# Packing W and transposed x into single buffers, aligning chunks at their ends, loading x for two tiles at once, in a store-heavy pairwise bilinear kernel

**Chip, cores, metric.** One core of a Trainium2 chip. The metric is the device time of one execution in microseconds (us). Ratios are the mean time of one kernel's fast runs over the mean of the other's fast runs of the same rounds, so they are not quite the ratio of the medians quoted here. A run counts as slow when it is over 1.5% above the fastest run of the same kernel.

## The reference

```python
# x = r_inputs: (4096, 32, 64) f32;  W: (496, 64, 64) f32, one matrix for each pair i < j of the 32 fields
i_idx, j_idx = np.triu_indices(32, k=1)
vi, vj = x[:, i_idx, :], x[:, j_idx, :]
y = (jnp.einsum('bpd,pde->bpe', vi, W) * vj).reshape(4096, -1)     # (4096, 31744) f32: 520 MB
```

The output is some twelve times larger than everything that is read, so almost all of the traffic is stores.

## The kernel before

The batch goes through in 32 tiles of 128 rows (one row a partition). Fields are taken in 16 pairs p = (2p, 2p+1), which share TensorE's array: the even field's x lies transposed on partitions 0 to 63, the odd one's on 64 to 127. For each pair, chunks of up to 512 columns are multiplied into two PSUM banks. VectorE multiplies both banks by x in one instruction of two runs, into a ring buffer in SBUF that holds 0.89 of a tile. Four stores a tile empty the ring.

```python
STORES = [[0, 1], [2, 3], [4, 5, 6], [7, 8, 9, 10, 11, 12, 13, 14, 15]]
...
for c0 in range(0, width[2 * p], CHUNK):            # CHUNK = 512; the short chunk comes last
    n = [max(0, min(CHUNK, width[2 * p + h] - c0)) for h in range(2)]
    half = -(-n[0] // BANK) * BANK
    pm = take_banks(2 * half // BANK)
    ...                                             # the matmuls of both fields
    o = [off[2 * p + h] - o0 + c0 for h in range(2)]
    xj = [(2 * p + h + 1) * D + c0 for h in range(2)]
    if n[1] > half - BANK and o[1] + n[0] <= store_w[s]:
        nc.vector.tensor_tensor(                    # both fields at once, n[0] columns each
            runs(osb, o[0], o[1], n[0]), runs(pm, 0, half, n[0]), runs(xt, xj[0], xj[1], n[0]), ALU.mult)
    else:
        ...                                         # one instruction for each field
...
nc.sync.dma_start(out=out[ts(t, P), o0 : o0 + store_w[s]], in_=osb)
```

Of the kernel before, what the change touches and what calls it, by code (L numbers as in the profile page):

```python
# [1 line left out]

# [6 lines left out]

F32 = mybir.dt.float32  # L10
ALU = mybir.AluOpType

P = 128
BANK = 512
BANKS = 8
CHUNK = BANK

STORES = [[0, 1], [2, 3], [4, 5, 6], [7, 8, 9, 10, 11, 12, 13, 14, 15]]
PREFETCH_AT = [5, 6]
RING = 28160  # L20


@with_exitstack
def pair_bilinear_kernel(
    ctx: ExitStack,
    tc: tile.TileContext,
    x: bass.AP,
    w: bass.AP,
    out: bass.AP,
    F: int,  # L30
    D: int,
):




















    nc = tc.nc
    B = x.shape[0]
    NT = B // P
    NPR = F // 2

    width = [(F - 1 - i) * D for i in range(F)]
    off = [sum(width[:i]) for i in range(F)]
    woff = [sum(width[0 : 2 * p : 2]) for p in range(NPR)]  # L60
    store_w = [sum(width[2 * p] + width[2 * p + 1] for p in g) for g in STORES]

    const = ctx.enter_context(tc.tile_pool(name="const", bufs=1))
    xtpool = ctx.enter_context(tc.tile_pool(name="xT", bufs=2))
    psum = ctx.enter_context(tc.tile_pool(name="ps", bufs=1, space=bass.MemoryType.PSUM))

    ident = const.tile([P, P], F32, tag="ident", name="ident")
    make_identity(nc, ident)

    def runs(tl, a, b, n):  # L70

        ap = tl[:, a : a + n]
        return bass.AP(ap.tensor, ap.offset, [list(ap.ap[0]), [b - a, 2], list(ap.ap[1])])


    xbuf = [const.tile([P, (F + 1) * D], F32, tag=f"x{b}", name=f"x{b}") for b in range(2)]
    for xb in xbuf:
        nc.gpsimd.memset(xb[:, F * D :], 0.0)  # L78

    def load_x(t):  # L80
        xt = xbuf[t % 2]
        nc.scalar.dma_start(out=xt[:, : F * D], in_=x[ts(t, P), :])
        return xt

    pring = psum.tile([P, BANKS * BANK], F32, tag="pring", name="pring")
    bank = 0

    def take_banks(n):

        nonlocal bank  # L90
        if bank + n > BANKS:
            bank = 0
        got = pring[:, bank * BANK : (bank + n) * BANK]
        bank = (bank + n) % BANKS
        return got

    def transpose_x(xT, t, xt, g):

        n = 2 * BANK // P
        pt = take_banks(2)  # L100
        for c in range(n):
            nc.tensor.transpose(pt[:, ts(c, P)], xt[:, ts(n * g + c, P)], ident)  # L102
        nc.scalar.copy(xT[:, ts(g, 2 * BANK)], pt)  # L103

    def new_xT(t):
        return xtpool.tile([P, NPR * P], F32, tag="xT", name=f"xT_{t}")

    ring = const.tile([P, RING], F32, tag="ring", name="ring")
    at = 0
    xs = {0: load_x(0)}  # L110

    w_sb = []
    for p in range(NPR):
        wp = const.tile([P, width[2 * p]], F32, tag=f"w{p}", name=f"w{p}")
        nc.sync.dma_start(out=wp, in_=w[:, woff[p] : woff[p] + width[2 * p]])
        w_sb.append(wp)

    xTs = {0: new_xT(0)}
    for g in range(2):
        transpose_x(xTs[0], 0, xs[0], g)  # L120

    for t in range(NT):
        xt, xT = xs.pop(t), xTs.pop(t)
        if t + 1 < NT:
            xs[t + 1] = load_x(t + 1)
        for s, group in enumerate(STORES):
            if at + store_w[s] > RING:
                at = 0
            osb = ring[:, at : at + store_w[s]]
            at += store_w[s]  # L130
            o0 = off[2 * group[0]]
            for p in group:
                if t + 1 < NT and p in PREFETCH_AT:
                    if t + 1 not in xTs:
                        xTs[t + 1] = new_xT(t + 1)
                    transpose_x(xTs[t + 1], t + 1, xs[t + 1], PREFETCH_AT.index(p))
                for c0 in range(0, width[2 * p], CHUNK):
                    n = [max(0, min(CHUNK, width[2 * p + h] - c0)) for h in range(2)]
                    half = -(-n[0] // BANK) * BANK
                    pm = take_banks(2 * half // BANK)  # L140
                    for b0 in range(0, n[0], BANK):
                        b1 = min(b0 + BANK, n[0])
                        for h in range(2):
                            if b0 < n[h]:
                                nc.tensor.matmul(  # L145
                                    pm[:, h * half + b0 : h * half + b1],
                                    xT[h * D : (h + 1) * D, ts(p, P)],
                                    w_sb[p][h * D : (h + 1) * D, c0 + b0 : c0 + b1],
                                    start=True,
                                    stop=True,  # L150
                                )
                    o = [off[2 * p + h] - o0 + c0 for h in range(2)]
                    xj = [(2 * p + h + 1) * D + c0 for h in range(2)]
                    if n[1] > half - BANK and o[1] + n[0] <= store_w[s]:
                        nc.vector.tensor_tensor(  # L155
                            runs(osb, o[0], o[1], n[0]),
                            runs(pm, 0, half, n[0]),
                            runs(xt, xj[0], xj[1], n[0]),
                            ALU.mult,
                        )  # L160
                    else:
                        for h in range(2):
                            if n[h]:
                                nc.vector.tensor_tensor(  # L164
                                    osb[:, o[h] : o[h] + n[h]],
                                    pm[:, h * half : h * half + n[h]],
                                    xt[:, xj[h] : xj[h] + n[h]],
                                    ALU.mult,
                                )
            nc.sync.dma_start(out=out[ts(t, P), o0 : o0 + store_w[s]], in_=osb)  # L170


# [33 lines left out]
```

## Time and profile before

| | before |
|---|---|
| time, median of 3 runs | 1337.8 us (1337.75 to 1338.07) |
| VectorE busy | 1199.1 us (90%) |
| TensorE matmuls busy | 1154.1 us (86%) |
| VectorE waiting for stores to free the ring | 68.0 us |
| moved by DMA | 562.88 MB, mean 421 GB/s |

The page's lines, the waits and a tile's end are shown in the prediction below.

### The profile page before, as it was taken

To read this page: it belongs to the slowest core of one execution; us is meant where nothing else is said; L and a number is where in the kernel's file an instruction comes from. 1 tells how busy PE (TensorE), PEld (TensorE's weight loads), DVE (VectorE), ACT (ScalarE), POOL (GpSimd) and SP (SyncE) were. 2 spreads that over 40 slices of the span, in tenths; PEclk is the share of its full clock that TensorE was granted. 3 is DMA by queue.
4 is the path that set the end of the run, shared out by engine and by line. 5 is a ranking of instruction groups with operands and counts; after the bars stand their busy time and mean duration, and the time that the engine had idled before them with its cause. 6 is when DMAs were issued, how large, how long until landed. Compare 5 with 4: busy or idle time off the path is not lost. (4 is left out here: it accounts for less than half of the span.)

```text
span 1335.8 us, 13084 instructions
## 1 busy us (share of the span) xinstructions
PE 1154.1 (86%) x5376; PEld 529.9 (40%) x5376; DVE 1199.1 (90%) x1344; ACT 66.1 (5%) x65; POOL 0.9 (0%) x8
## 2 busy tenths in 40 slices
PE   7898898988888889898888898898988888888883
PEld 3343343433343444344334444343443333333331
DVE  5999898999899999899999899989988989999994
ACT  1000000000000000000000000000000000000000
POOL 0000000000000000000000000000000000000000
PEclk9999999899999999999999999999999999999997
DMA  9999999999999999999999999999999999999998
GB/s 392 435 426 431 436 408 434 415 426 431 419 417 425 428 429 416 418 424 420 424 436 419 418 421 426 424 426 421 418 430 414 426 423 413 424 427 430 418 420 370
DMA packets 25403, 562.88 MB, mean 421 GB/s; under 512 B 2944, under 2 KB 3328, under 8 KB 4864
## 3 DMA queue, kind: packets, MB, share of 16 engines
q1 hardware_dynamic: 20736, 528.49, 92.6%
q10 hardware_dynamic: 4608, 33.56, 6.0%
q8 instruction: 42, 0.69, 0.2%
q14 instruction: 17, 0.14, 0.0%
HBM read 41.94 MB, written 520.09 MB: 421 GB/s over the span
## 5 line engine op out<-in xcount | busy, mean ns | idle before, releaser
L155 DVE TENSOR_TENSOR ring<-pring,x 128x1024 f32<-128x1024 f32 (+3 forms) x1088 | 1154.2, 1107 | 116.9 <-DMA out_dram<-ring 68.0
L145 PE MATMUL pring<-w,xT 64*128 64x512 f32 (+4 forms) x4864 | 1087.8, 563 | 132.3 <-DVE ring L155 127.9
L145 PEld LDWEIGHTS pring<-w,xT 64*128 64x128 f32 x4864 | 472.9, 192 | 721.4 <-DVE ring L155 611.7
L103 ACT COPY xT<-pring 128x1024 f32<-128x1024 f32 x64 | 64.8, 1012 | 1197.1 <-PE pring L102 1197.1
L102 PE MATMUL pring<-ident,x 128*128 128x128 f32 x512 | 71.5, 285 | 30.7 <-DMA x<-in_x_dram 30.3
L102 PEld LDWEIGHTS pring<-ident,x 128*128 128x128 f32 x512 | 57.0, 144 | 65.6 <-issue 65.6
L164 DVE TENSOR_TENSOR ring<-pring,x 128x64 f32<-128x64 f32 (+4 forms) x256 | 70.9, 297 | 3.3
L103 ACT ACT_TABLE_LOAD x1 | 1.3, 1283 | 1.7 <-PEq L198 1.7
masks.py:199 POOL TENSOR_SCALAR_AFFINE_SELECT ident<-ident 128x128 f32<-128x128 f32 x1 | 0.3, 292 | 0.0
L78 POOL MEMSET x<- 128x64 f32 x2 | 0.2, 152 | 0.0
masks.py:197 POOL MEMSET ident<- 128x128 f32 x1 | 0.2, 204 | 0.3 <-POOLq L198 0.3
L198 POOL MEMSET const-bfloat16-1.0<- 128x1 bf16 x1 | 0.1, 101 | 0.0
L198 POOL MEMSET const-uint8-127<- 128x1 uint8 x1 | 0.1, 101 | 0.0
L198 POOL MEMSET const-float32-0.0<- 128x1 f32 x1 | 0.1, 98 | 0.2 <-issue 0.2
L198 POOL MEMSET const-float32-1.0<- 128x1 f32 x1 | 0.1, 98 | 0.0
## 6 DMA issues: line engine op xcount, KB each, us to landing
out_dram<-ring SPq DMA_DIRECT2D x32, 4896.0 KB, 18.6
out_dram<-ring SPq DMA_DIRECT2D x32, 3936.0 KB, 17.4
out_dram<-ring SPq DMA_DIRECT2D x32, 3776.0 KB, 19.0
out_dram<-ring SPq DMA_DIRECT2D x32, 3264.0 KB, 19.4
x<-in_x_dram ACTq DMA_DIRECT2D x32, 1024.0 KB, 17.8
w<-in_w_dram SPq DMA_DIRECT2D x1, 992.0 KB, 7.5
w<-in_w_dram SPq DMA_DIRECT2D x1, 928.0 KB, 11.8
w<-in_w_dram SPq DMA_DIRECT2D x1, 864.0 KB, 13.4
```

Of the source, the lines that this page charges most:

```text
L78: nc.gpsimd.memset(xb[:, F * D :], 0.0)
L102: nc.tensor.transpose(pt[:, ts(c, P)], xt[:, ts(n * g + c, P)], ident)
L103: nc.scalar.copy(xT[:, ts(g, 2 * BANK)], pt)
L145: nc.tensor.matmul(pm[:, h * half + b0 : h * half + b1], xT[h * D : (h + 1) * D, ts(p, P)], w_sb[p][h * D : (h + 1) * D, c0 + b0 : c0 + b1 ...
L155: nc.vector.tensor_tensor(runs(osb, o[0], o[1], n[0]), runs(pm, 0, half, n[0]), runs(xt, xj[0], xj[1], n[0]), ALU.mult,)
L164: nc.vector.tensor_tensor(osb[:, o[h] : o[h] + n[h]], pm[:, h * half : h * half + n[h]], xt[:, xj[h] : xj[h] + n[h]], ALU.mult,)
L198: nc = bacc.Bacc("TRN2", target_bir_lowering=False, num_devices=1)
```

## The change

It packs W into one SBUF buffer filled by five loads, keeps one transposed-x buffer whose two halves are refilled in turn (at pair 3 for the current tile, at pair 9 for the next), loads x for two tiles with one DMA, lays the batch out so that each partition owns 32 consecutive rows, and puts the short chunk of each pair first, so that all chunks end where the pair ends. With W's odd rows shifted by one block of zeros, both fields use the same columns of x. The intent is fewer, larger transfers and fewer exceptions in VectorE's work. The core of the diff:

```diff
-PREFETCH_AT = [5, 6]
+LOADS = [[0], [1], [2, 3], [4, 5, 6], [7, 8, 9, 10, 11, 12, 13, 14, 15]]
+FIRST_HALF_AT, SECOND_HALF_AT = 9, 3
+def x_slots(NT): ...                 # tile 0 alone, then pairs of tiles, in three slots of one buffer
-    for p in range(NPR):
-        wp = const.tile([P, width[2 * p]], F32, tag=f"w{p}", name=f"w{p}")
-        nc.sync.dma_start(out=wp, in_=w[:, woff[p] : woff[p] + width[2 * p]])
+    w_sb = const.tile([P, sum(width[0::2])], F32, tag="w", name="w")
+    for g in LOADS:
+        upto = woff[2 * g[-1]] + width[2 * g[-1]]
+        nc.sync.dma_start(out=w_sb[:, done:upto], in_=w[:, done:upto])
...
-                for c0 in range(0, width[2 * p], CHUNK):
+                first = (width[2 * p] - 1) % BANK + 1
+                for c1 in range(first, width[2 * p] + 1, BANK):
+                    n = first if c1 == first else BANK
+                    c0 = c1 - n
+                    odd = width[2 * p + 1] and c1 > D
...
+                    o = [off[2 * p + h] - o0 + c0 - h * D for h in range(2)]
+                    if odd and (c0 or c1 < width[2 * p]):
                         nc.vector.tensor_tensor(
-                            runs(xt, xj[0], xj[1], n[0]),
+                            bass.AP(xj.tensor, xj.offset, [xj.ap[0], [0, 2], xj.ap[1]]),
...
-            nc.sync.dma_start(out=out[ts(t, P), o0 : o0 + store_w[s]], in_=osb)
+            nc.sync.dma_start(
+                out=out[:, t * cols + o0 : t * cols + o0 + store_w[s]], in_=osb
+            )
...
+    rows = r_inputs.reshape(P, NT, F * D)
-    o_d = nc.dram_tensor("out_0_dram", (B, NP * D), F32, kind="ExternalOutput").ap()
+    o_d = nc.dram_tensor("out_0_dram", (P, NT * NP * D), F32, kind="ExternalOutput").ap()
```

More of the change, by code (lines that the diff above doesn't have):

```diff
@@ L15, with x_slots @@
 BANKS = 8
-CHUNK = BANK
 STORES = [[0, 1], [2, 3], [4, 5, 6], [7, 8, 9, 10, 11, 12, 13, 14, 15]]
-PREFETCH_AT = [5, 6]
+LOADS = [[0], [1], [2, 3], [4, 5, 6], [7, 8, 9, 10, 11, 12, 13, 14, 15]]
+FIRST_HALF_AT, SECOND_HALF_AT = 9, 3
 RING = 28160
+def x_slots(NT):
+    loads = [[(0, 0)]]
+    for t in range(1, NT, 2):
+        if t + 1 == NT:
+            loads.append([(t, 1)])
+        elif loads[-1][-1] == (t - 1, 2):
+            loads.append([(t + 1, 0), (t, 1)])
+        else:
+            loads.append([(t, 1), (t + 1, 2)])
+    return loads
 @with_exitstack
@@ L53, in pair_bilinear_kernel @@
     nc = tc.nc
-    B = x.shape[0]
-    NT = B // P
+    NT = out.shape[1] * 2 // (F * (F - 1) * D)
     NPR = F // 2
@@ L59, in pair_bilinear_kernel @@
     off = [sum(width[:i]) for i in range(F)]
-    woff = [sum(width[0 : 2 * p : 2]) for p in range(NPR)]
+    cols = sum(width)
+    woff = [i % 2 * D + sum(width[i % 2 : i : 2]) for i in range(F)]
     store_w = [sum(width[2 * p] + width[2 * p + 1] for p in g) for g in STORES]
     const = ctx.enter_context(tc.tile_pool(name="const", bufs=1))
-    xtpool = ctx.enter_context(tc.tile_pool(name="xT", bufs=2))
     psum = ctx.enter_context(tc.tile_pool(name="ps", bufs=1, space=bass.MemoryType.PSUM))
@@ L73, in runs, with load_x @@
         return bass.AP(ap.tensor, ap.offset, [list(ap.ap[0]), [b - a, 2], list(ap.ap[1])])
-    xbuf = [const.tile([P, (F + 1) * D], F32, tag=f"x{b}", name=f"x{b}") for b in range(2)]
-    for xb in xbuf:
-        nc.gpsimd.memset(xb[:, F * D :], 0.0)
-    def load_x(t):
-        xt = xbuf[t % 2]
-        nc.scalar.dma_start(out=xt[:, : F * D], in_=x[ts(t, P), :])
-        return xt
+    xbuf = const.tile([P, 3 * F * D], F32, tag="x", name="x")
+    x_loads = x_slots(NT)
+    slot = {t: xbuf[:, ts(s, F * D)] for load in x_loads for t, s in load}
+    def load_x(load):
+        at = sum(len(before) for before in x_loads[: x_loads.index(load)]) * P * F * D
+        n = len(load) * F * D
+        s = load[0][1]
+        nc.scalar.dma_start(
+            out=xbuf[:, s * F * D : s * F * D + n],
+            in_=x[at : at + P * n].rearrange("(p c) -> p c", p=P),
+        )
     pring = psum.tile([P, BANKS * BANK], F32, tag="pring", name="pring")
@@ L95, in take_banks, with transpose_x @@
         return got
-    def transpose_x(xT, t, xt, g):
+    xT = const.tile([P, NPR * P], F32, tag="xT", name="xT")
+    def transpose_x(xt, g):
         n = 2 * BANK // P
@@ L103, in transpose_x @@
         nc.scalar.copy(xT[:, ts(g, 2 * BANK)], pt)
-    def new_xT(t):
-        return xtpool.tile([P, NPR * P], F32, tag="xT", name=f"xT_{t}")
     ring = const.tile([P, RING], F32, tag="ring", name="ring")
     at = 0
-    xs = {0: load_x(0)}
-    w_sb = []
-    for p in range(NPR):
-        wp = const.tile([P, width[2 * p]], F32, tag=f"w{p}", name=f"w{p}")
-        nc.sync.dma_start(out=wp, in_=w[:, woff[p] : woff[p] + width[2 * p]])
-        w_sb.append(wp)
-    xTs = {0: new_xT(0)}
-    for g in range(2):
-        transpose_x(xTs[0], 0, xs[0], g)
+    load_x(x_loads[0])
+    w_sb = const.tile([P, sum(width[0::2])], F32, tag="w", name="w")
+    done = 0
+    for g in LOADS:
+        upto = woff[2 * g[-1]] + width[2 * g[-1]]
+        nc.sync.dma_start(out=w_sb[:, done:upto], in_=w[:, done:upto])
+        done = upto
+    transpose_x(slot[0], 0)
     for t in range(NT):
-        xt, xT = xs.pop(t), xTs.pop(t)
-        if t + 1 < NT:
-            xs[t + 1] = load_x(t + 1)
+        xt = slot[t]
+        for load in x_loads:
+            if min(load)[0] == t + 1:
+                load_x(load)
         for s, group in enumerate(STORES):
@@ L132, in pair_bilinear_kernel @@
             for p in group:
-                if t + 1 < NT and p in PREFETCH_AT:
-                    if t + 1 not in xTs:
-                        xTs[t + 1] = new_xT(t + 1)
-                    transpose_x(xTs[t + 1], t + 1, xs[t + 1], PREFETCH_AT.index(p))
-                for c0 in range(0, width[2 * p], CHUNK):
-                    n = [max(0, min(CHUNK, width[2 * p + h] - c0)) for h in range(2)]
-                    half = -(-n[0] // BANK) * BANK
-                    pm = take_banks(2 * half // BANK)
-                    for b0 in range(0, n[0], BANK):
-                        b1 = min(b0 + BANK, n[0])
-                        for h in range(2):
-                            if b0 < n[h]:
-                                nc.tensor.matmul(
-                                    pm[:, h * half + b0 : h * half + b1],
-                                    xT[h * D : (h + 1) * D, ts(p, P)],
-                                    w_sb[p][h * D : (h + 1) * D, c0 + b0 : c0 + b1],
-                                    start=True,
-                                    stop=True,
-                                )
-                    o = [off[2 * p + h] - o0 + c0 for h in range(2)]
-                    xj = [(2 * p + h + 1) * D + c0 for h in range(2)]
-                    if n[1] > half - BANK and o[1] + n[0] <= store_w[s]:
@@ new lines, in pair_bilinear_kernel @@
+                if p == SECOND_HALF_AT:
+                    transpose_x(xt, 1)
+                if p == FIRST_HALF_AT and t + 1 < NT:
+                    transpose_x(slot[t + 1], 0)
+                first = (width[2 * p] - 1) % BANK + 1
[3 more added lines that the diff above has]
+                    odd = width[2 * p + 1] and c1 > D
+                    pm = take_banks(2)
+                    for h in range(1 + bool(odd)):
+                        a = woff[2 * p + h] + c0 - h * D
+                        nc.tensor.matmul(
+                            pm[:, h * BANK : h * BANK + n],
+                            xT[h * D : (h + 1) * D, ts(p, P)],
+                            w_sb[h * D : (h + 1) * D, a : a + n],
+                            start=True,
+                            stop=True,
+                        )
+                    xj = xt[:, (2 * p + 1) * D + c0 : (2 * p + 1) * D + c1]
+                    o = [off[2 * p + h] - o0 + c0 - h * D for h in range(2)]
+                    if odd and (c0 or c1 < width[2 * p]):
@@ L155, in pair_bilinear_kernel @@
                         nc.vector.tensor_tensor(
-                            runs(osb, o[0], o[1], n[0]),
-                            runs(pm, 0, half, n[0]),
-                            runs(xt, xj[0], xj[1], n[0]),
+                            runs(osb, o[0], o[1], n),
+                            runs(pm, 0, BANK, n),
+                            bass.AP(xj.tensor, xj.offset, [xj.ap[0], [0, 2], xj.ap[1]]),
                             ALU.mult,
@@ L161, in pair_bilinear_kernel @@
                     else:
-                        for h in range(2):
-                            if n[h]:
-                                nc.vector.tensor_tensor(
-                                    osb[:, o[h] : o[h] + n[h]],
-                                    pm[:, h * half : h * half + n[h]],
-                                    xt[:, xj[h] : xj[h] + n[h]],
-                                    ALU.mult,
-                                )
-            nc.sync.dma_start(out=out[ts(t, P), o0 : o0 + store_w[s]], in_=osb)
+                        for h in range(1 + bool(odd)):
+                            nc.vector.tensor_tensor(
+                                osb[:, o[h] + h * D : o[h] + n],
+                                pm[:, h * (BANK + D) : h * BANK + n],
+                                xj[:, h * D :],
+                                ALU.mult,
+                            )
+            nc.sync.dma_start(
+                out=out[:, t * cols + o0 : t * cols + o0 + store_w[s]], in_=osb
+            )
 def kernel(r_inputs, L0_rec_W):
@@ L179 @@
     NP = L0_rec_W.shape[0]
-    x = np.ascontiguousarray(r_inputs).reshape(B, F * D)
+    NT = B // P
+    rows = r_inputs.reshape(P, NT, F * D)
+    x = np.concatenate([rows[:, [t for t, _ in load]].ravel() for load in x_slots(NT)])
     wt = np.transpose(L0_rec_W, (1, 0, 2))
@@ L185 @@
     first = [sum(n[:i]) for i in range(F)]
-    halves = [
-        np.concatenate(
-            [
-                np.pad(wt[:, first[i] : first[i] + n[i]], ((0, 0), (0, h), (0, 0)))
-                for i in range(h, F, 2)
-            ],
-            axis=1,
-        )
-        for h in range(2)
-    ]
-    w = np.ascontiguousarray(np.stack(halves)).reshape(2 * D, -1)
+    w = np.zeros((2, D, sum(n[0::2]), D), wt.dtype)
+    for h in range(2):
+        of_h = [wt[:, first[i] : first[i] + n[i]] for i in range(h, F, 2)]
+        w[h, :, h : h + sum(n[h::2])] = np.concatenate(of_h, axis=1)
+    w = w.reshape(2 * D, -1)
     nc = bacc.Bacc("TRN2", target_bir_lowering=False, num_devices=1)
@@ L204 @@
     r = run_bass_kernel_spmd(nc, [{"in_x_dram": x, "in_w_dram": w}], core_ids=[0])
-    return r.results[0]["out_0_dram"]
+    return r.results[0]["out_0_dram"].reshape(B, NP * D)
```

## The prediction

> **What bounds the kernel now.** I read the views in this order: the page, the chain of waits, short windows at a tile's end, and then the trace's single DMA packet records. The page comes first because it shows which resource never rests.
>
> ```profile
> span 1335.8 us, 13084 instructions
> PE 1154.1 (86%) x5376; PEld 529.9 (40%) x5376; DVE 1199.1 (90%) x1344; ACT 66.1 (5%) x65; POOL 0.9 (0%) x8
> ...
> DVE  5999898999899999899999899989988989999994
> ...
> DMA  9999999999999999999999999999999999999998
> ...
> q1 hardware_dynamic: 20736, 528.49, 92.6%
> q10 hardware_dynamic: 4608, 33.56, 6.0%
> ```
>
> VectorE (DVE) is busy for 90%, but the DMA row has a 9 in every slice but the last: the queues' shares add to 98.8% of 16 engines' span. So the transfers are the first suspect. The waits say who holds whom up.
>
> ```profile
> PEld pring L145 <- DVE ring L155: 611.7, 935, 1.9
> PE pring L145 <- DVE ring L155: 127.9, 215, 1.7
> DVE ring L155 <- DMA out_dram<-ring: 68.0, 35, 3.0
> PE pring L102 <- DMA x<-in_x_dram: 30.3, 23, 8.5
> DVE ring L155 <- PE pring L145: 16.7, 7, 13.6
> DVE ring L155 <- DVE ring L155: 0.9, 2, 0.5
> ```
>
> (Columns: who waits for whom, us in total, times, longest.) TensorE waits for VectorE, VectorE waits for the stores to free the ring (68.0 us, about 2.1 us a tile), and nothing waits for TensorE except once, 13.6 us, at the start. The transposes wait 30.3 us for x, and none of that reaches VectorE. So the order is DMA, then VectorE close behind, then TensorE.
>
> Yet DMA is not perfectly full. Here is the end of one tile, in windows (columns: the stretch, then busy times of PE, PEld, DVE, ACT, POOL, the clock, the DMA share, GB/s):
>
> ```profile
> 407.00:417.00 10.00, 8.16 (x43) 3.64 (x43) 9.70 (x12) 0.00 (x0) 0.00 (x0) 1.00 1.01 435
> ...
> 419.00:420.00 1.00, 1.00 (x6) 0.46 (x6) 0.90 (x3) 0.00 (x0) 0.00 (x0) 1.00 0.29 126
> 420.00:421.00 1.00, 1.00 (x8) 0.41 (x6) 1.00 (x2) 0.00 (x0) 0.00 (x0) 1.00 1.70 611
> ```
>
> (A packet is booked where it starts or overlaps, so single microseconds go over 1.) There is a hole of about half a microsecond just before the last and largest store (4896 KB) of each tile is issued at 419.74. The packet records show who idles: 14 of the engines end the 3936 KB store at 420.03 to 420.17 and then have nothing queued, but the last one ends it at 423.97. It never runs dry. On that engine a store packet takes longer: 31,488-byte packets average about 1193 ns there against a mode of 1166 over all engines, 30,208-byte ones 1155 against 1119, so some 2 to 3%; its x packets are at the common 309 ns. As each store is complete only with its slowest engine, **one slow DMA engine, busy from about 2 us to 1334.5 us, sets the time.**
>
> Its work adds up. Modal packet times per tile: (968 + 1119 + 1166 + 1448) ns x 8 rows = 37.6 us of stores and 8 x 309 ns = 2.5 us of x; times 32 tiles that is 1282.6 us. W adds 8 x 2.57 us = 20.5 us (the sum of the modal times of the 16 row sizes), semaphore packets 1.6 us: 1304.7 us. The slow engine's 2.25% on 1203.5 us of stores adds 27 us: 1332. The span has 2 us before and 1.3 us after it.
>
> **What the Trainium skill says.** (1) "DMA: Bandwidth & Descriptors", section "Where 436 GB/s comes from": 16 ports at 27.2 GB/s each make 435.2 GB/s. The trace agrees: 435 in the window above, and a 26,112-byte packet in 968 ns is 26.97 GB/s. So the ordinary engines have nothing left to win. (2) The same page, "Latency and other measured facts": engines 7 and 15 are usually slower than the others, with a cause that it calls a guess and ties to GpSimd-issued DMA. The trace has one slower engine although all DMAs here are issued by SP and ACT; it does not tell its number. (3) The same section: HBM row pitches at large powers of two lose rate: 207 GB/s a direction at 512 KiB, 164 at 2 MiB, 103 at 4 MiB, against 214 for a padded 4 MiB. The kernel before has a pitch of 126,976 bytes (31 x 4 KiB), so its trace cannot show this. (4) "VectorE: DVE Perf Modes", "The TRN2 errata": an fp32 tensor_tensor takes (N + 151)/0.96 ns, 1224 ns for N = 1024; the rows by form give 1217.
>
> **The change part by part.**
>
> *x for two tiles at once.* 17 loads in place of 32. Bytes stay, rows of 8 KB become 16 KB. From the store packets the slope is (1119 - 968)/4096 ns a byte, which leaves about 7 ns fixed for each packet (309 - 302). Half of the x packets of 30 tiles go: 120 per engine x 7 ns = 0.8 us. A 2 MB load lies beside the big store, as the 1 MB load does now (17.8 us to landing); every second tile then gets 2.5 us more x and the others 2.5 us less. In a tile without x the slow engine needs 38.5 us, and VectorE needs 37.5 us busy plus about 1.2 us of small gaps (137 idle, less 68.0, 13.6 at the start and 16.8 at the end, over 32), so 38.7: it comes to the ring wait up to 0.7 us late. The slow engine has about 4 us of queue left when the big store is issued (423.97 less 419.74), so it does not run dry. The loads are needed only at pair 9, some 33 us into a tile, so the 30.3 us of PE waits should vanish, worth nothing.
>
> *One packed W, five loads.* 11 descriptors fewer for each row: 11 x 8 x 7 ns = 0.6 us per engine, with the semaphores 0.9 us. At the start W now shares the engines with 2 MB of x rather than 1 MB; the second pair's W lands perhaps 3 us later, but only one group of transposes precedes the matmuls. Either way loads and stores are queued back to back, so the DMA engines' sum stays.
>
> *Chunks aligned at their ends.* Counting the loops: before, 34 double and 8 single VectorE instructions per tile (1088 and 256 over 32); after, 33 and 10, as pairs 12 to 14 always split, and pairs 1, 3 and 6 lose or keep their exception. Forms: 1024 stays at 24; one 896 of the four (1079 ns) turns into 448 + 384, at 1.03 ns an element plus some 150 ns (from the single rows: 216 ns at 64, 480 at 320) 612 + 546 = 1158 ns. That is +0.08 us a tile, **+2.5 us of VectorE in all**, against 68.0 us that it waits for stores: hidden. The x operand read twice from one address keeps its element count. TensorE keeps 4864 matmuls; 12 odd-row ones per tile have 64 columns more, but run beside their even twins and in 128 us of waiting for VectorE: hidden.
>
> *One transposed-x buffer.* 64 ACT copies and 512 transposes stay, at other places; the first half is written after the last matmul that reads it, in the same engine's order. 0.
>
> *Layout.* Each partition owns 32 consecutive rows of the batch, so the store's row pitch in HBM goes from 124 KiB to 31 x 128 KiB. Packet count and size stay. Sum if the rate stays: 0.
>
> Sum: -0.8 - 0.9 = -1.7 us on the slow engine, 1336.1 us. I lower this by 1 us for the small chance that the layout helps that engine: **1335 us**.
>
> **The rivals.** (a) *The new pitch costs rate.* For: it is a multiple of 128 KiB, and rows four partitions apart are 31 x 512 KiB apart. Against: 31 is odd, 2^17 is a smaller power than that of the 512 KiB case, which lost only 3%. If the stores lost 3%: +36 us, 1372. (b) *The new addresses free the slow engine.* For: its reads are not slow, only its writes. Against: the slowness stays on over all tiles, each with other addresses, which looks like the engine and not the address. It would take off at most 27 us, less what the next slowest engine has from instruction fetches (42 packets, 0.69 MB, on several engines): some 1312 us, -1.9%. (c) *VectorE becomes the bound*, if aligned chunks, whose first chunk writes 64 columns that a later one overwrites, bring waits of VectorE on itself. Before has two of these, 0.9 us. It would take over 0.2 us for each of the 9 such chunks a tile to use up 68 us; I expect under 20 us, hidden, at most 1345.
>
> **Range and chances.** Most likely 1330 to 1339, as the DMA work hardly changes. Below, (b) in part; above, (a) or (c) in part: **1318 to 1346** for 8 in 10. Over 2% faster means below 1311, which needs (b) in full and more: **0.04**. Over 2% slower means above 1364.6, which needs (a): **0.08**. Within 2%: **0.88**.
>
> **What would show it.** Right: the DMA row still full, some 422 GB/s, 2448 packets (17 x 144) on the x queue, 1376 VectorE instructions, VectorE's wait for stores near 65 us, no wait for x on the transposes, the slow engine's packets still 2% long. Wrong: modal store packets over 968 and 1448 ns (a), the slow engine's packets at the mode (b), waits of VectorE on VectorE or on TensorE in place of the 68 us (c), or a dry slow engine in tiles without x.

## More of the kernel before

The odd field is 64 columns narrower than the even one. In a pair's last chunk the joint instruction still writes n[0] columns for both, so it writes 64 spare columns past the odd field's end. These are the first 64 columns of the next pair, and the next pair's first chunk overwrites them.

## The result, and the profile after

The kernel after took 1336.78 us (median of 6 runs, 1336.64 to 1336.90), and before took 1337.95 us beside it (6 runs, 1337.75 to 1338.13). The ratio is 0.9991, 95% interval 0.9978 to 1.0004: the same within 2%. If anything it is 1.2 us faster, and the interval includes no change.

The page of the kernel after, its lines that answer to those shown of before:

```profile
span 1335.1 us, 13080 instructions
PE 1160.6 (87%) x5376; PEld 544.9 (41%) x5376; DVE 1183.4 (89%) x1376; ACT 66.1 (5%) x65; POOL 0.7 (0%) x6
...
DMA  9999999999999999999999999999999999999998
...
q1 hardware_dynamic: 19152, 528.49, 92.8%
q10 hardware_dynamic: 2448, 33.56, 5.9%
```

The bytes are the same, the x queue has 2448 packets instead of 4608, and the DMA row is as full as before. VectorE has 32 instructions more (1376) and yet 16 us **less** busy time. The waits of the kernel after (who for whom, us in total, times, longest; PEld is TensorE's weight load, pring the PSUM banks, L180 the multiplication of both fields at once, L188 that of one field):

```profile
PEld pring L170 <- DVE ring L180: 533.0, 754, 6.4
...
PE pring L170 <- DVE ring L180: 133.5, 162, 5.9
DVE ring L180 <- DMA out_dram<-ring: 102.6, 44, 6.2
DVE ring L180 <- PE pring L170: 17.9, 9, 13.5
...
PE pring L130 <- DMA x<-in_x_dram: 8.6, 1, 8.6
...
DVE ring L188 <- DMA out_dram<-ring: 1.9, 1, 1.9
```

TensorE's waits for x are gone but for the one at the start (30.3 before, 8.6 after), and the time is the same. VectorE's wait for stores went from 68.0 to 102.6 + 1.9 = 104.5 us. So VectorE became some 36 us quicker, and it spends all of this waiting for the same stores.

Where does it come from? The timeline of before, first tile: a short joint chunk (2 x 448 columns) and the first chunk of the next pair (columns: start us, us, engine, line and operation):

```profile
17.02 1.08 DVE L155 TENSOR_TENSOR ring<-pring,x 128x896 f32<-128x896 f32 x1
...
18.20 1.22 DVE L155 TENSOR_TENSOR ring<-pring,x 128x1024 f32<-128x1024 f32 x1
```

The first ends at 17.02 + 1.08 = 18.10, and the next starts 0.10 us after that. In the timeline of after a short chunk (2 x 320) stands first in its pair and is followed by a chunk that it doesn't overlap:

```profile
18.41 0.82 DVE L180 TENSOR_TENSOR ring<-pring,x 128x640 f32<-128x640 f32 x1
...
19.14 1.22 DVE L180 TENSOR_TENSOR ring<-pring,x 128x1024 f32<-128x1024 f32 x1
```

Here the next starts at 19.14, before the first ends at 19.23. That is the usual case: from the records of all VectorE instructions, the next one normally starts 83 ns before the one in front ends. A start 60 to 130 ns *after* its end, so some 185 ns lost, occurs 309 times in before (57 us in all) and 67 times in after (12.5 us). This window misses some of after. With each record placed in the kernel's loops, the rule is exact: in before, 320 instructions overwrite columns that the one just in front has written (10 a tile), and none of them starts early; in after there are 96 (the short chunks of pairs 8 to 10, each with only one chunk behind it), all late, 31 of them by some 133 ns, outside the window. So the loss went from some 59 us to 19 us. Of the starts without such an overlap, 2 of 1023 in before and 7 of 1279 in after come 60 to 200 ns late.

No line of the waits view shows it; that view has only 0.9 us of VectorE on VectorE for before. But the trace records what it is: in 309 of the 320 cases of before, and in all 96 of after, a semaphore instruction of VectorE stands between the two, which waits for the semaphore that VectorE's own multiplications raise. The late start is thus a wait in the compiled program (the other 11 lack the record; they start 90 ns after the end). Such a wait without an overlap, 192 times in after, delays nothing: the next instruction starts 84 ns before the end as usual (median).

The single instructions did not get shorter. Their durations add up to 1283.4 us after and 1280.2 us before; the busy time fell because an instruction that starts late no longer overlaps the one in front.

The packets of the DMA engines look much as they did (those of 26,112 bytes average 974 ns, 972 before). The lagging engine is still there: its 26,112-byte packets average some 994 ns in both kernels, against the common 968. Big stores are now issued some 38 to 39 us apart in a tile without x and 42 to 44 us apart in a tile with x. At the tile's end that stood in the prediction the hole is there too (windows of after; columns as there: stretch, busy times, clock, DMA share, GB/s):

```profile
418.00:419.00 1.00, 1.00 (x8) 0.72 (x7) 1.00 (x4) 0.00 (x0) 0.00 (x0) 1.00 0.17 71
419.00:420.00 1.00, 1.00 (x8) 0.67 (x6) 1.00 (x2) 0.00 (x0) 0.00 (x0) 1.00 1.99 619
```

The big store was issued at 418.46, and the lagging engine ended the store in front of it only at 423.13.

### The profile page after: what moved, and what is told of

It reads as the page before. It is cut to its first block, busy times and chain, and to the rows that moved or that the text cites. A ratio compares the mean times of both kernels' runs of the same rounds, so it can differ in the third digit from the quotient of the medians.

```text
span 1335.1 us, 13080 instructions
## 1 busy us (share of the span) xinstructions
PE 1160.6 (87%) x5376; PEld 544.9 (41%) x5376; DVE 1183.4 (89%) x1376; ACT 66.1 (5%) x65; POOL 0.7 (0%) x6
## 3 DMA queue, kind: packets, MB, share of 16 engines
q10 hardware_dynamic: 2448, 33.56, 5.9%
## 4 chain that ended last, share of the span: by engine, by line
DMA 47%; DVE 38%; issue 9%; PE 5%; DVEq 0%; ACT 0%
DMA out_dram<-ring 46%; DVE ring L180 32%; DVE ring L188 5%; PE pring L170 5%; DMA x<-in_x_dram 1%; DVEq L180 0%; PE pring L130 0%; ACT xT L131 0%; DVEq L225 0%; DVEq L188 0%
## 5 line engine op out<-in xcount | busy, mean ns | idle before, releaser
L180 DVE TENSOR_TENSOR ring<-pring,x 128x1024 f32<-128x1024 f32 (+3 forms) x1056 | 1104.1, 1108 | 131.4 <-DMA out_dram<-ring 102.6
L170 PEld LDWEIGHTS pring<-w,xT 64*128 64x128 f32 x4864 | 489.3, 191 | 711.7 <-DVE ring L180 533.0
L188 DVE TENSOR_TENSOR ring<-pring,x 128x64 f32<-128x64 f32 (+3 forms) x320 | 97.7, 356 | 2.6 <-DMA out_dram<-ring 1.9
## 6 DMA issues: line engine op xcount, KB each, us to landing
out_dram<-ring SPq DMA_DIRECT2D x32, 3936.0 KB, 18.1
x<-in_x_dram ACTq DMA_DIRECT2D x15, 2048.0 KB, 20.4
```

What stands on the lines that cost most here:

```text
L170: nc.tensor.matmul(pm[:, h * BANK : h * BANK + n], xT[h * D : (h + 1) * D, ts(p, P)], w_sb[h * D : (h + 1) * D, a : a + n], start=True, st ...
L180: nc.vector.tensor_tensor(runs(osb, o[0], o[1], n), runs(pm, 0, BANK, n), bass.AP(xj.tensor, xj.offset, [xj.ap[0], [0, 2], xj.ap[1]]), ALU ...
L188: nc.vector.tensor_tensor(osb[:, o[h] + h * D : o[h] + n], pm[:, h * (BANK + D) : h * BANK + n], xj[:, h * D :], ALU.mult,)
```

## The experiments

**Theory:** the DMA engines' work, to be exact that of the slowest engine, sets the time; the change leaves this work nearly as it was, makes VectorE faster, and the gain is hidden behind the stores. **Rivals:** VectorE or TensorE sets the time; the aligned chunks did nothing for VectorE; the new layout cost or gave something that another part made up for; the limit is the total rate and not one engine.

### 1. Fewer partitions stored: a failed experiment

To relieve the stores I stored 112 or 120 of the 128 partitions (wrong results), in three kernels with 112: after, before, and before with each pair's chunks reversed (explained under 2).

```diff
-                out=out[:, t * cols + o0 : t * cols + o0 + store_w[s]], in_=osb
+                out=out[:112, t * cols + o0 : t * cols + o0 + store_w[s]], in_=osb[:112, :]
```

> The kernel after, but only partitions 0 to 111 are stored (wrong result on purpose): every DMA engine has 7 rows a store instead of 8. My theory (the DMA engines set the time, VectorE was made faster and hides it): the DMA work falls by about an eighth of 1230 us, so VectorE becomes the bound, and the time falls by about what VectorE waited for stores, 104.5 us, to some 1225 to 1240 us, below the same cut of the kernel before by about 37 us. Rival (VectorE or TensorE, not the stores, already sets the time): 1330 us or more. Rival (aligned chunks did nothing for VectorE): the same time as the cut kernel before.

> The kernel before, storing partitions 0 to 111 only (wrong result on purpose). My theory: VectorE-bound, 1338 less its 68 us of waits for stores: 1260 to 1275 us, some 2.5 to 3% above the cut kernel after, because its VectorE loses about 185 ns whenever a shortened last chunk is followed at once by the next pair's first chunk, which overwrites its 64 spare columns (61 us in all in its trace, 21 us after). Rival (no such gain): both cut kernels within 0.5% of each other.

> The kernel before with the chunks of each pair taken from the last to the first, so that the chunk that overwrites the spare columns no longer follows at once, and the stores cut to 112 partitions (wrong result on purpose). If the 185 ns are a wait on the overlapping write: 8 of the 10 short chunks a tile lose it, some 45 us, so 1220 to 1235 us, near the cut kernel after. If they come from the access pattern or the sizes of the chunks: 1260 to 1275 us, as the cut kernel before.

> The kernel after, storing partitions 0 to 119 only (wrong result on purpose), which should put 8 rows on each of 15 DMA engines and none on the sixteenth. Theory of one slow engine: if the sixteenth is the slow one, all the others run at the common packet times and the time falls by most of its 27 us, to 1305 to 1315 us; if the slow one is among the 15, it still has the same 8 rows, and the time stays at 1333 to 1338 us with one lagging engine in the packets. Rival (the limit is the total rate of all engines, 435 GB/s or HBM): a sixteenth of the bytes less makes it some 75 us faster, down to VectorE's bound of about 1235 us.

Measured medians: 1810.8, 1808.8, 1765.0 and 1817.0 us, where before took 1337.8: a third slower with *less* to store, and wide (1720 to 1856 us). The runs counted as fast took 1730.1, 1759.7 and 1719.8 us (one each) and 1783.7 and 1788.4 us. Every expectation missed. The page of the kernel after with 112 partitions (a slow run, as are the profiles of the other three):

```profile
DMA  9876887876888778796878877787876887877885
...
DMA packets 19611, 497.86 MB, mean 276 GB/s; under 512 B 2400, under 2 KB 2400, under 8 KB 2656
```

Packets of 39,168 bytes took 1898 ns on average with 112 partitions and 2221 ns with 120, against 1480 in before. With 112 all 16 engines took part (2128 semaphore packets, with which an engine reports its share of a transfer done: 128 stores x 16 + 5 W loads x 16), with 120 only 15 (2000 = 128 x 15 + 80). Why the packets got slow stays open: no run shows which rows an engine gets. The cut says nothing about VectorE, and nothing about which engine lags.

### 2. Fewer columns stored

The same relief without touching the partitions: all 128, but only the first 7/8 of each group's columns (wrong).

```diff
-                out=out[:, t * cols + o0 : t * cols + o0 + store_w[s]], in_=osb
+                out=out[:, t * cols + o0 : t * cols + o0 + store_w[s] * 7 // 8],
+                in_=osb[:, : store_w[s] * 7 // 8],
```

> The kernel after, all 128 partitions stored but only the first 7/8 of each group's columns (wrong result on purpose): the DMA packets are an eighth shorter and keep their engines. The cut to 112 or 120 partitions went wrong (1730 to 1856 us, packets up to twice as long), so this takes its place. My theory (stores set the time, a faster VectorE hides behind them): VectorE becomes the bound, 1336.8 less its 104.5 us of waits: 1222 to 1240 us. Rival (VectorE or TensorE already sets the time): above 1320 us.

> The kernel before with the same cut of the columns (wrong result on purpose). My theory: 1338 less 68 us of waits for stores: 1260 to 1275 us, some 3% over the cut kernel after, as its VectorE loses about 185 ns at each of 10 short chunks a tile. Rival (the aligned chunks changed nothing on VectorE): within 0.5% of the cut kernel after.

The third kernel is before with this cut and a change of order alone:

```diff
-                for c0 in range(0, width[2 * p], CHUNK):
+                for c0 in reversed(range(0, width[2 * p], CHUNK)):
```

> The kernel before with the same cut and with each pair's chunks taken from last to first, so that the chunk that overwrites the spare columns does not follow at once (wrong result on purpose only by the cut). If the 185 ns are a wait on that overlapping write, most of them go: 1215 to 1235 us, near the cut kernel after. If they come from sizes or patterns, which stay the same: 1260 to 1275 us.

| stores cut to 7/8 | median us (4 runs, all fast) | late starts (60 to 130 ns) |
|---|---|---|
| after | 1217.24 (1217.03 to 1217.58) | 66 |
| before | 1258.81 (1258.34 to 1259.20) | 311 |
| before, chunks reversed | 1227.91 (1226.18 to 1230.93) | 94 |

The three pages in the order of the table, one line each:

```profile
PE 1138.1 (94%) x5376; PEld 522.8 (43%) x5376; DVE 1177.7 (97%) x1376; ACT 66.1 (5%) x65; POOL 0.7 (0%) x6
```

```profile
PE 1119.4 (89%) x5376; PEld 501.8 (40%) x5376; DVE 1196.3 (95%) x1344; ACT 66.1 (5%) x65; POOL 0.9 (0%) x8
```

```profile
PE 1107.9 (90%) x5376; PEld 504.3 (41%) x5376; DVE 1179.3 (96%) x1344; ACT 66.1 (5%) x65; POOL 0.9 (0%) x8
```

VectorE at 95 to 97% of the span is now the bound, and the waits for stores have all but gone (1.1 us in the cut kernel after). So in the full kernels it was the stores that held VectorE up: a cut of the stores alone takes 120 us off the kernel after and 79 us off before. And **here the change is worth 41.6 us, 3.3%** (1258.81 to 1217.24), about the 40 us by which the late starts fell. This is the gain that the full kernel hides. (Both cut kernels came out just below their ranges, by 5 and 1 us.)

The reversed order tells what it is. Instructions, sizes and patterns are those of before. What differs on VectorE is that the chunk with the 64 spare columns is mostly no longer followed at once by the chunk that overwrites them (TensorE's order changes along with it), and 217 of 311 late starts go, and 30.9 us with them. The 94 that stay are all in pairs 12 to 14, which have a single chunk, so that the overwriting one still comes next. 217 times 185 ns would be 40 us; a part was not gained, as VectorE's waits for TensorE rose from 17.4 to 27.1 us. At the same size (2 x 192 columns, then 2 x 512) the timeline of this kernel shows no loss:

```profile
22.09 0.55 DVE L155 TENSOR_TENSOR ring<-pring,x 128x384 f32<-128x384 f32 x1
...
22.55 1.22 DVE L155 TENSOR_TENSOR ring<-pring,x 128x1024 f32<-128x1024 f32 x1
```

The second starts before the first ends (22.64). In before this pair of sizes stands 647 ns apart on average, here 465 ns.

### 3. The order alone, stores whole

> The kernel before with only the order of each pair's chunks reversed; nothing is cut, the result is right. My theory: VectorE gets some 30 us or more faster (as in the cut kernels, 1258.8 against 1227.9), its wait for stores grows from 68 us to 95 us or more, and the time stays within 0.15% of before. Rival (VectorE's speed sets the time): 20 to 30 us faster.

Measured: 1338.04 us (4 runs, correct), ratio 1.0002 (0.9985 to 1.0018). VectorE was 13.4 us less busy (1185.7 against 1199.1), and the time did not move. This shows on a correct kernel that a gain on VectorE is worth nothing while the stores set the pace. Its waits:

```profile
DVE ring L155 <- DMA out_dram<-ring: 72.1, 28, 3.6
PE pring L102 <- DMA x<-in_x_dram: 62.6, 31, 8.7
...
DVE ring L155 <- PE pring L145: 29.3, 54, 13.3
DVE ring L164 <- DMA out_dram<-ring: 9.9, 13, 1.3
DVE ring L164 <- PE pring L145: 6.9, 11, 0.9
DVE ring L155 <- PE pring L102: 5.2, 2, 2.8
```

The wait for stores rose less than expected, to 72.1 + 9.9 = 82.0 us. VectorE also waited more for TensorE (41.4 us in all its lines, 19.2 before), and the transposes waited longer for x (62.6 us against 30.3); which of the two brought the other is not shown. So of the time that VectorE gained, 14 us went into waits for stores and 22 us into waits for TensorE.

### 4. The layout alone undone

```diff
-    rows = r_inputs.reshape(P, NT, F * D)
+    rows = r_inputs.reshape(NT, P, F * D).transpose(1, 0, 2)
-                out=out[:, t * cols + o0 : t * cols + o0 + store_w[s]], in_=osb
+                out=out[ts(t, P), o0 : o0 + store_w[s]], in_=osb
```

> The kernel after with the layout alone undone: a tile is again 128 consecutive rows of the batch, and the output's row pitch is 126,976 bytes instead of 4,063,232. My theory (the layout is neutral, as packets run at the engines' rate with either): within 0.15% of the kernel after, so 0.998 to 1.0005 of before, and the same slow engine. Rival (the layout cost or gave something that another part of the change made up for): a ratio below 0.996 or above 1.003.

Measured: 1336.87 us (5 runs), ratio 0.9994 (0.9981 to 1.0006); the kernel after has 0.9991. The layout is neutral within this resolution.

### 5. A row pitch of exactly 4 MiB

```diff
-    o_d = nc.dram_tensor("out_0_dram", (P, NT * NP * D), F32, kind="ExternalOutput").ap()
+    o_d = nc.dram_tensor("out_0_dram", (P, 1 << 20), F32, kind="ExternalOutput").ap()
```

> The kernel after with its output rows padded to a pitch of exactly 4 MiB in HBM (the padding is sliced off on the host; the result is right). My theory, from the Trainium skill's table of row pitches: the pitch of 31 x 128 KiB was harmless because 31 is odd; at 4 MiB the store packets should take two to four times as long and the kernel 2500 to 5000 us. Rival (the pitch never matters to stores from SBUF): 1337 us.

Measured: 2126.4 us, correct (one run, state unknown, so only the size of it counts).

```profile
DMA  9999999999999999999999999999999999999998
...
DMA packets 21659, 562.87 MB, mean 265 GB/s; under 512 B 2400, under 2 KB 2400, under 8 KB 2656
```

The packets are as many as in after, but those of 26,112 bytes have a median of 1673 ns instead of 968. So the pitch does matter to stores from SBUF, though less than expected, and the change came within a padding of 128 KiB a row of taking 59% longer. The DMA row reads as full as ever: it counts slow packets as busy, and only GB/s tells them apart.

### 6. Extra work for one DMA engine

An extra write of 48,960 bytes to a scratch tensor, 31 times: in the one kernel from one partition, shaped as 17 pieces so that a single engine carries it; in the control, the same 1.5 MB from all partitions.

```diff
+        if t > 0:
+            src = w_sb[0:1, :12240]
+            nc.scalar.dma_start(
+                out=extra[:, t * 736 : t * 736 + 720],
+                in_=bass.AP(src.tensor, src.offset, [list(src.ap[0]), [720, 17], [1, 720]]))
```

```diff
+        if t > 0:
+            nc.scalar.dma_start(out=extra[:, ts(t, 96)], in_=w_sb[:, :96])
```

> The kernel after plus, in 31 of 32 tiles, one more write of 48,960 bytes in 17 pieces from one partition to a scratch tensor in HBM, shaped so that a single DMA engine carries it. At some 2880 bytes in about 113 ns a piece that is 1.9 us a tile on that engine, 60 us in all, and 1.5 MB in total (0.3% of the bytes). Theory of the slowest engine: if it falls on the slow engine, +55 to +65 us; if on an ordinary one, that has some 27 us less to do, +25 to +40 us. Rival (total rate of all engines is the limit): +3 to +6 us.

> Control: the kernel after plus a write of the same 1.5 MB in all from all 128 partitions (384 bytes each, 8 pieces on every engine, some 0.2 us a tile). Both theories: +4 to +8 us, and so it shows that the extra write's place on one engine, not its bytes or its waits, is what the other run measures.

Measured: 1404.91 us on one engine, 1352.59 us on all (4 runs each, correct), so +68.1 and +15.8 us over after's 1336.78. Both lie above the expected ranges. The runs did not do quite what I wrote: the compiled programs did not issue one extra write a tile. The control issued all 31 between 10 and 44 us, within its first tile; the other issued them between 31 and 501 us, over its first twelve. That is where the control's +15.8 instead of 4 to 8 comes from: its first two slices moved 357 and 348 GB/s instead of 397 and 433, and later tiles have the old spacing.

On one engine, the twelve tiles from the first big store on took 553 us where after needs 490, so 63 us more, and later tiles have the old spacing. The 527 pieces of 118 ns are 62 us on one engine; the control's 3968 pieces of 22 ns are 5.5 us on each of sixteen. So the sum fits. The waits fit less well. The run with one engine:

```profile
DVE ring L187 <- DMA out_dram<-ring: 103.5, 32, 6.8
DVE ring L187 <- PE pring L177: 79.0, 56, 19.2
...
PE pring L131 <- DMA x<-in_x_dram: 35.9, 3, 18.5
```

What grew against after is VectorE's wait for TensorE (79.6 us in all its lines, 18.1 in after) more than its wait for stores (110.5 against 104.5). The extra writes go through the x queue, the transposes waited 35.9 us for x against 8.6, and one load of x took 41.6 us to land, against a median of 20.4 in after. So the difference of the two runs, **52.3 us for the same bytes**, may be the place of the work or x that came late, and the writes also fell at different times. That one engine's work sets the time is not settled by it. The run can't say either whether it hit the lagging engine.

## Why the prediction was right, and where it was not

- **The bound** (shown). Stores set the time: with an eighth of the columns cut, both kernels fall to VectorE's rate; with VectorE faster alone, nothing moves (1.0002). TensorE held VectorE up for 5.6 us in before beyond the wait at the start (16.7 + 2.5 - 13.6), not for nothing as the prediction read it, but this is too little to matter.
- **One slow engine** (argued, not shown). The packets show one engine 2 to 3% slow in its writes, in every full kernel looked at and with both layouts. The test with extra work on one engine fits, but late x is a rival for it. The other engines are nearly full as well (the queues' shares add to 98.8%), so a limit on all of them differs from a limit on this one by some 2% at most, and no run separates the two. Which engine it is and why its writes are slow stays open; the attempt to leave an engine out failed. The prediction's reading of the tile's end is also a little off: 12 engines, not 14, ended the store by 420.17, 14 by 420.47, and a second straggler at 421.73, before the last at 423.97.
- **The sum, -1.7 us and another -1 us for the layout, 1335 us.** Measured 1336.8, a change of -1.2 us, within its interval of zero. The packet counts came as worked out (2448). The saving of some 7 ns a packet was not tested alone, and the 1 us for the layout was not seen (experiment 4), so that the sum comes within 2 us of the measured time proves none of its small terms.
- **x for two tiles** (right). The slow engine did not run dry in tiles without x (4.8 us left at the big store issued at 461.66), tiles took some 38.5 and 43.4 us by turns, and the waits for x vanished without effect.
- **Layout** (right): neutral. The 4 MiB run shows that rival (a), the cost of a pitch, had real ground.
- **The step that failed: "+2.5 us of VectorE in all".** The count of instructions was right (1376), and so was the sum of their durations (+3.2 us, 1280.2 to 1283.4), but the cost of the order was left out. I took the view's "DVE <- DVE 0.9 us, 2 times" to say that before had hardly any waits of VectorE on itself, and feared in rival (c) that the change would bring some. In fact before had 320 late starts of some 185 ns, and the change left 96: VectorE gained about 40 us. Hence the wrong mark for its wait for stores (near 65 us, measured 104.5). The time came out right because this whole gain is hidden, not because it was foreseen.

No run with a correct result was faster than the kernel after by more than noise. While the stores set the pace, a faster VectorE wins nothing in this form, as the runs show. Fewer bytes would help; whether a cure for the lagging engine would, no run shows.

## What to carry to other kernels

Before pricing an engine's work, ask what ends its idle time; if it is a DMA queue that is always full, a real gain of 3% on that engine can be worth nothing, and cutting the transfers on purpose is the way to see it. Look at start-to-start times and not only at the waits: a joint instruction that writes some columns too many costs a late start, here some 185 ns, if the very next one overwrites them, because the compiled program then waits between the two, and a change of order is enough to avoid it. When testing, cut transfers by columns: the cut by partitions made these stores slower. And check the row pitch of what is stored: exactly 4 MiB took 59% longer here, 31 x 128 KiB nothing.

## What the Trainium skill lacked or had wrong

- "DMA: Bandwidth & Descriptors" and "SBUF — State Buffer": neither gives the cost of storing 112 or 120 partitions (the second has rates for 4, 16, 32, 64 and 128). In fast runs 112 took 1720 to 1760 us in three kernels and 120 some 1786 us, against 1337 for all 128. The number of engines agrees with the first page, "Why a DMA increments its semaphore by 16 and not by 1": by its rule, the largest number up to 16 that divides the partitions, 112 go to 16 engines and 120 to 15, as the semaphore packets show.
- "DMA: Bandwidth & Descriptors", "Latency and other measured facts", row pitch: its 103 GB/s at 4 MiB is for copies between HBM tensors; stores from SBUF kept a mean of 265 GB/s (reads of x included). A pitch of 31 x 128 KiB, which it doesn't list, lost nothing (0.9991 against 0.9994 with 124 KiB).
- The same section ties usually slow DMA engines to GpSimd-issued DMA, as a guess. Here one engine was 2 to 3% slow in writes (994 against 968 ns) with all DMAs issued by SP and ACT, and not in reads (309 ns for x before). The trace doesn't tell its number.
- "VectorE: DVE Perf Modes": its duration for fp32 tensor_tensor holds (1224 ns by the formula, 1217 measured). A row of such instructions goes at 1131 ns from start to start. The page's "The DRAIN you can't avoid" finds no extra cost for a semaphore after each instruction (8 copies took as long with one after each as with one after the last); here a wait for the semaphore of the multiplication just in front moved the start from 83 ns before its end to 104 ns after it, about 185 ns.
